# Moving the next graph's node matrix behind conv 1's node product in a two-layer graph network kernel

## The chip, the core and the metric

The kernel runs on one core of one Trainium2 chip. The time is the device time of one execution in microseconds (us). The matrix engine is TensorE (PE, with PEld for its weight loads); the others are VectorE (DVE), ScalarE (ACT), GpSimd (POOL) and the queue of SyncE (SP), which issues the transfers (DMA).

## What is computed

There are 128 graphs. Each has 128 nodes with 512 features (`x`, float32) and a 128x128 adjacency matrix `adj`. Layer 0 is a pair of hypergraph convolutions with a layer norm between them, layer 1 a mean aggregation; both have a layer norm in front and add their result to `x`. Cut to what matters:

```
h = max(layernorm(x), 0)
H = (adj != 0);  w = first row of adj                 # per graph
Dn = 1 / (H @ w);  Be = 1 / column sums of H          # 0 where the sum is 0
conv(v, W, b) = Dn * (H @ (Be * (H.T @ (v @ W.T)))) + b
y = conv(layernorm(relu(conv(h, W1, b1))) * gamma + beta, W2, b2)     # 512 -> 1024 -> 512
x = x + (y + h)
h = max(layernorm(x), 0)
x = x + relu(concat(h, adj @ h / rowsum(adj)) @ W.T)
```

The kernel forms `S = H Be H.T`, a 128x128 matrix of a graph (the **node matrix**), together with the sums `H @ w` as one more column. Conv 1 first multiplies `S` with the features (the **node product**), and then with the weights.

## The kernel before

All weights stay on chip. A product with weights is made of three products of rounded parts (high, low and a correction, letters `h`, `l`, `d`), so that TensorE's faster float32 form can be used; helper `product` (L521) issues them, each with 512 columns, into two PSUM banks (`...m` and `...d`). A pool of six banks serves these, another of two serves the small products `ps_s` (node matrix) and `pz` (node product).

The work of a graph is cut into some eighty small stages (functions under `@stage`), each called with the graph's number. The order of the calls is written out by hand: `head` for the first graphs, `step(s)` for s from 3 to 124, `tail` for the last. Every engine works off its instructions in the order of the calls; a call that waits holds up what is behind it on the same engine only. In one step several graphs are under way: conv 1 of graph s and the start of s + 1, conv 2 of s - 1 and s - 2, layer 1 of s - 3 and s - 4, and the preparation of s + 2. On TensorE a step is, in this order: node matrix of s + 1, second half of conv 1's weights of s (`rm`, `rd`), conv 2's node product of s - 2 (`ym`, `yd`), layer 1's mean weights (`bm`, `bd`), node product of s + 1 (`pz`), layer 1's self weights (`am`, `ad`), conv 2's weights of s - 1 (`gm`, `gd`), the aggregate (into `am`, `ad`), first half of conv 1's weights of s + 1.

The names that the change touches:

- The node matrix's operands come from a chain of small stages. `load_adjb` fetches the adjacency block by block (four transfers on SP's queue), `incidence` (L386) transposes it (`raw`) and compares it with 0 (`adjt`) on DVE, with the column sums; `incidence_weight`, `incidence_count` and `incidence_inverse` prepare two columns (`cnt`), `incidence_high` splits them into high and low, and two calls of `incidence_scale` scale `adjt` by them into `sb`. `node_matrix` multiplies `adjt` and `sb` (258 columns) and copies the first half of the result to `s` on ACT; `node_sum` adds the second half on DVE; `node_floor`, `node_scale` and `node_up` make the factors `dinv` from the last column.
- `conv1_nodes` (L485) issues four products of 128 columns in plain float32, `x_norm` makes its feature operand `h`; `conv1_high`, `conv1_low` and `conv1_rest` split the result into the three parts `z`.
- Layer 1 transposes its input through memory: `layer1_trip_out` writes `h_scratch`, `layer1_trip_in` reads it back in four transfers as `hb`, `layer1_turn` transposes blocks on DVE (`ht`). Conv 2's input goes the same way (`n_scratch`, `nb`, `nt`), and the mean operator (`an_scratch`, `anb`). `finish` makes the output `o` on DVE, `store` sends it out.
- `fill` puts float32 products of constants in front of the next small product, `w1[..].high/low/rest` and `scale_w2` prepare weights in the head.

In the step of before, the node matrix of s + 1 is called early, with operands that were prepared in the middle and at the end of the step before it.

Of the kernel before, what the change touches and what calls it, by code (L numbers as in the profile page):

```python
# [24 lines left out]
def gnn_kernel(  # L25
# [401 lines left out]
    @stage  # L427
    def node_matrix(g):
        PS[g] = ps = small_bank("ps_s")
        nc.tensor.matmul(ps[:, : 2 * P + 2], HT.pop(g), SB.pop(g)[:, : 2 * P + 2], start=True, stop=True)  # L430
        s = small.tile([P, P + 1], FP, tag="s", name="s", bufs=4)
        copy(s, ps[:, : P + 1], AF.Copy, scale=4096.0 if steady(g) else 1.0)
        S[g] = s

# [49 lines left out]
    @stage  # L484
    def conv1_nodes(g):  # L485
        PZ[g] = z = small_bank("pz")
        for k in range(KD):
            nc.tensor.matmul(z[:, k * P : (k + 1) * P], H0[g][:, k * P : (k + 1) * P], S[g],  # L488
                             start=True, stop=True)

# [365 lines left out]
    def step(s):  # L856
        node_high(s - 2)
        conv2_bias(s - 2)
        conv2_high(s - 2)
        layer1_self_main(s - 4)  # L860
        layer1_high(s - 3)
        inner_out(s - 1)
        conv2_low(s - 2, nc.vector)
        x_norm(s + 1)
        node_rest(s - 2)
        conv1_main(s, 0)
        layer1_self_out(s - 4)
        conv2_rest(s - 2)
        node_matrix(s + 1)
        conv1_weights(s, 1)  # L870
        conv1_out(s, 0)
        mean_out(s - 3)
        layer1_low(s - 3)
        layer1_rest(s - 3)
        inner_in(s - 1)
        conv2_nodes(s - 2)
        node_sum(s + 1)
        node_floor(s + 1, nc.gpsimd)
        conv2_out(s - 2)
        conv1_main(s, 1)  # L880
        conv1_out(s, 1)
        inner_turn(s - 1)
        layer1_sums(s - 2)
        mean_in(s - 3)
        layer1_spread(s - 2)
        conv1_bias(s, 0)
        load_adj(s - 2)
        incidence(s + 2)
        layer1_mean(s - 3)
        incidence_weight(s + 2, nc.vector)  # L890
        scales(s - 2, 3)
        layer1_mean_main(s - 3)
        finish(s - 4)
        conv1_bias(s, 1)
        shifts(s - 2, 3, nc.vector)
        conv1_nodes(s + 1)
        store(s - 4)
        load_x(s + 2)
        inner_high(s - 1)
        conv1_high(s + 1)  # L900
        mean_transpose(s - 3)
        layer1_mean_out(s - 3)
        layer1_self(s - 3)
        mean_operator(s - 2)
        inner_low(s - 1, nc.vector)
        inner_rest(s - 1)
        layer1_norm(s - 2)
        inner_sums(s)
        layer1_mean_high(s - 3)
        inner_spread(s)  # L910
        conv2_weights(s - 1)
        layer1_mean_low(s - 3, nc.vector)
        node_scale(s + 1)
        mean_rest(s - 3)
        layer1_trip_out(s - 2)
        x_sums(s + 2)
        incidence_count(s + 2, nc.vector)
        mean_degree(s - 2, nc.vector)
        conv2_main(s - 1)
        scales(s, 2)  # L920
        layer1_mean_rest(s - 3)
        layer1_trip_in(s - 2)
        conv1_low(s + 1)
        incidence_inverse(s + 2)
        residual(s + 1)
        mean_inverse(s - 2)
        conv2_weights_out(s - 1)
        conv1_rest(s + 1)
        shifts(s, 2, nc.gpsimd)
        load_adjb(s + 3)  # L930
        inner_norm(s)
        incidence_high(s + 2)
        layer1_turn(s - 2)
        x_spread(s + 2)
        aggregate(s - 3)
        mean_scale(s - 2, nc.vector)
        incidence_scale(s + 2, 0, nc.vector)
        scales(s + 2, 1)
        conv1_weights(s + 1, 0)
        incidence_scale(s + 2, 1, nc.vector)  # L940
        shifts(s + 2, 1, nc.vector)
        residual_bias(s + 1)
        node_up(s + 1, nc.vector)

    def head():
        load_w1(0, 0)
        load_adjb(0, nc.scalar)
        load_x(1)
        incidence(0)
        copy(eps_root, eps, AF.Sqrt)  # L950
        load_affine()
        load_x(0)
        incidence_weight(0, nc.gpsimd)
        incidence_count(0, nc.vector)
        load_w1(0, 1)
        incidence_inverse(0)
        x_sums(1, "A")
        x_sums(0)
        w1[0].high(0)
        w1[0].high(1)  # L960
        load_x(2)
        load_w1(1, 0)
        w1[0].low(0)
        incidence_high(0)
        x_spread(0)
        scales(0, 1)
        incidence_scale(0, 0, nc.gpsimd)
        incidence_scale(0, 1, nc.scalar)
        load_w1(1, 1)
        w1[0].low(1)  # L970
        w1[0].rest(1, nc.vector)
        load_adjb(1)
        shifts(0, 1, nc.gpsimd)
        x_norm(0)
        node_matrix(0)
        fill(768)
        w1[1].high(1)
        load_w2(0)
        node_sum(0)
        incidence(1)  # L980
        conv1_nodes(0)
        w1[1].high(0)
        residual(0)
        node_floor(0, nc.vector)
        incidence_count(1, nc.vector)
        load_adjb(2)
        w1[0].rest(0, nc.vector)
        x_spread(1)
        load_bias(b2_bc, b2)
        load_bias(b1_bc, b1)  # L990
        w1[1].low(1)
        incidence_inverse(1)
        conv1_high(0)
        conv1_low(0)
        conv1_rest(0)
        node_scale(0)
        incidence_weight(1, nc.gpsimd)
        conv1_weights(0, 0)
        incidence_high(1)
        w1[1].low(0)  # L1000
        incidence_scale(1, 0, nc.scalar)
        w1[1].rest(0, nc.vector)
        incidence_scale(1, 1, nc.scalar)
        load_adj(0)
        node_up(0, nc.scalar)
        conv1_main(0, 0)
        scales(1, 1)
        load_w2(1)
        node_matrix(1)
        shifts(1, 1, nc.gpsimd)  # L1010
        incidence(2)
        node_sum(1)
        incidence_count(2, nc.gpsimd)
        beta_row(0)
        conv1_out(0, 0)
        w1[1].rest(1, nc.vector)
        x_sums(2)
        beta_row(1)
        conv1_weights(0, 1)
        incidence_weight(2, nc.vector)  # L1020
        node_floor(1, nc.gpsimd)
        x_spread(2)
        scale_w2(0, nc.vector)
        scales(2, 1)
        x_norm(1)
        beta_row(2)
        load_x(3)
        shifts(2, 1, nc.gpsimd)
        incidence_inverse(2)
        conv1_bias(0, 0, nc.vector)  # L1030
        scale_w2(1, nc.scalar)
        w2[0].high(0)
        beta_row(3)
        incidence_high(2)
        conv1_nodes(1)
        load_adjb(3)
        scale_w2(2, nc.vector)
        conv1_main(0, 1)
        load_w3(1)
        mean_operator(0)  # L1040
        node_scale(1)
        scale_w2(3, nc.scalar)
        incidence_scale(2, 0, nc.vector)
        incidence_scale(2, 1, nc.scalar)
        w2[0].high(1)
        conv1_out(0, 1)
        residual_bias(0)
        conv1_high(1, True)
        node_matrix(2)
        conv1_bias(0, 1, nc.vector)  # L1050
        beta_row(4)
        beta_row(5)
        x_norm(2)
        node_sum(2)
        conv1_nodes(2)
        mean_degree(0, nc.vector)
        node_up(1, nc.gpsimd)
        node_floor(2, nc.vector)
        inner_sums(0)
        inner_spread(0)  # L1060
        residual(1)
        node_scale(2)
        residual(2)
        load_adjb(4)
        conv1_low(1)
        scale_w2(5, nc.vector)
# [3 lines left out]
        incidence_weight(3, nc.gpsimd)  # L1070
        conv1_rest(1)
        incidence_count(3, nc.gpsimd)
        scales(0, 2)
        incidence_inverse(3)
        conv1_low(2)
        beta_row(6)
        shifts(0, 2, nc.vector)
        beta_row(7)
        w2[1].high(0)
        conv1_rest(2)  # L1080
        incidence_high(3)
        w2[0].low(1)
        unit()
        scale_w2(6, nc.vector)
        inner_norm(0)
        x_sums(3)
        scale_w2(7, nc.scalar)
        w2[0].low(0)
        mean_inverse(0)
        w2[1].low(0)  # L1090
        node_up(2, nc.scalar)
        incidence_scale(3, 0, nc.vector)
        w2[1].high(1)
        conv1_weights(1, 0)
        conv1_weights(1, 1)
        incidence_scale(3, 1, nc.scalar)
        conv1_main(1, 0)
        conv1_main(1, 1)
        inner_out(0)
        w2[0].rest(0)  # L1100
        inner_in(0)
        conv1_out(1, 0)
        x_spread(3)
        w2[0].rest(1)
        conv1_out(1, 1)
        conv1_bias(1, 0, nc.vector)
        conv1_bias(1, 1, nc.vector)
        inner_sums(1)
        node_matrix(3)
        conv1_weights(2, 0)  # L1110
        scales(3, 1)
        incidence(4)
        w2[1].low(1)
        inner_spread(1)
        w2[1].rest(1, nc.gpsimd)
        incidence_weight(4, nc.vector)
        load_x(5)
        inner_turn(0)
        beta_out()
        scales(1, 2)  # L1120
        conv1_weights(2, 1)
        incidence_count(4, nc.gpsimd)
        inner_high(0)
        shifts(1, 2, nc.scalar)
        node_sum(3)
        inner_norm(1)
        w3[1].high(1)
        w3[1].high(0)
# [432 lines left out]
```

## Time and profile before

| what | value |
| --- | --- |
| median of 3 runs (lowest to highest) | 2449.39 us (2448.46 to 2452.33) |
| the profiled execution | 2447.67 us |
| its span, from first to last instruction | 2445.9 us |
| granted TensorE clock | 1.0 |
| node matrix `ps_s`, TensorE | 128 products of 258 columns |
| node product `pz`, TensorE | 1024 records of 128 columns |
| HBM traffic over the span | 126 GB/s |

A profile is one execution. Its page gives the busy time of each engine, the span in 40 slices, the chain of waits that ended last, and groups of equal instructions. The time line gives instructions in order of their start, equal ones merged (x4 is four of them), with the start in us from the span's start. Records of a matrix product overlap, since products are pipelined, so what one costs is read from its start to the start of the next. The windows view gives the busy time of all engines in a stretch.

### The profile page before, as it was taken

To read this page: it belongs to the slowest core of one execution; us is meant where nothing else is said; L and a number is where in the kernel's file an instruction comes from. 1 tells how busy PE (TensorE), PEld (TensorE's weight loads), DVE (VectorE), ACT (ScalarE), POOL (GpSimd) and SP (SyncE) were. 2 spreads that over 40 slices of the span, in tenths; PEclk is the share of its full clock that TensorE was granted. 3 is DMA by queue.
4 is the path that set the end of the run, shared out by engine and by line. 5 is a ranking of instruction groups with operands and counts; after the bars stand their busy time and mean duration, and the time that the engine had idled before them with its cause. 6 is when DMAs were issued, how large, how long until landed. Compare 5 with 4: busy or idle time off the path is not lost.

```text
span 2445.9 us, 41647 instructions
## 1 busy us (share of the span) xinstructions
PE 2422.7 (99%) x11170; PEld 2009.6 (82%) x11170; DVE 2298.1 (94%) x5843; ACT 2009.9 (82%) x4512; POOL 1324.8 (54%) x1808
## 2 busy tenths in 40 slices
PE   7999999999999999999999999999999999999998
PEld 5788888888888888888888888888888888888886
DVE  8899999999999999999999999999999999999987
ACT  8888888888888888888888888888888888888785
POOL 5555555555555555555555555555555555555552
PEclk9999999999999999999999999999999999999999
DMA  6344433344434443444344443434343444344432
GB/s 186 114 129 125 130 124 129 124 130 128 129 119 130 132 126 123 129 129 127 124 128 128 126 129 123 132 123 130 122 133 121 130 127 131 119 131 131 127 124 92
DMA packets 408956, 311.39 MB, mean 127 GB/s; under 512 B 176656, under 2 KB 339984, under 8 KB 408720
## 3 DMA queue, kind: packets, MB, share of 16 engines
q1 hardware_dynamic: 407888, 308.66, 40.1%
q8 instruction: 88, 1.44, 0.2%
q14 instruction: 148, 1.21, 0.2%
q10 hardware_dynamic: 576, 0.07, 0.0%
q0 software_dynamic: 256, 0.01, 0.0%
HBM read 166.21 MB, written 142.34 MB: 126 GB/s over the span
## 4 chain that ended last, share of the span: by engine, by line
PE 95%; ACT 2%; DVE 1%; DMA 1%; issue 1%; SPq 0%; POOL 0%; POOLq 0%; DVEq 0%; ACTq 0%
PE gm L530 19%; PE rm L530 18%; PE am L530 9%; PE bm L530 9%; PE gd L535 9%; PE rd L535 9%; PE bd L535 5%; PE ad L535 5%; PE pz L488 4%; PE am L832 2%; PE ad L832 1%; PE ym L743 1%; PE yd L744 1%; PE ym L742 1%; PE ps_s L430 1%
## 5 line engine op out<-in xcount | busy, mean ns | idle before, releaser
L306 ACT ACTIVATE h<-x_t 128x512 f32<-128x512 f32 x255 | 159.1, 624 | 291.8 <-DVE x_t L754 283.8
L81 POOL TENSOR_TENSOR r<-r,b_bc 128x256 f32<-128x256 f32 x500 | 358.7, 739 | 70.1 <-DVE r L555 54.4
L300 POOL TENSOR_SCALAR st<-st 128x1 f32<-128x1 f32 x130 | 82.3, 633 | 569.9 <-DVE st L317 563.2
L81 POOL TENSOR_TENSOR hl<-ht,hh 128x256 fp32r<-128x256 f32 x250 | 235.4, 963 | 216.5 <-ACT hh L612 216.5
L81 POOL TENSOR_TENSOR x_t<-x_t,h 128x256 f32<-128x256 f32 x256 | 239.8, 959 | 1.3 <-ACT h L326 1.1
L81 POOL TENSOR_TENSOR g<-g,c 128x256 f32<-128x256 f32 x246 | 177.6, 743 | 72.4 <-DVE g L694 72.4
L326 ACT ACTIVATE h<-x_t,st 128x512 f32<-128x512 f32 x255 | 206.1, 808 | 2.0 <-POOL st L300 1.2
L555 DVE SCALAR_TENSOR_TENSOR r<-rd,dinv,r 128x512 f32<-128x512 f32 x256 | 190.8, 746 | 7.7 <-ACT r L550 6.3
L81 POOL TENSOR_TENSOR x_t<-x_t,b_bc 128x256 f32<-128x256 f32 x256 | 187.2, 752 | 0.0
L311 ACT ACTIVATE h<-x_t,st 128x512 f32<-128x512 f32 x255 | 182.9, 717 | 4.1
L550 ACT ACTIVATE r<-rm,dinv 128x512 f32<-128x512 f32 x256 | 174.7, 684 | 7.7 <-PE rm L530 4.4
L694 DVE SCALAR_TENSOR_TENSOR g<-gd,g 128x512 f32<-128x512 f32 x127 | 87.8, 691 | 79.5 <-issue 70.4
L621 DVE SCALAR_TENSOR_TENSOR nd<-nh,nl 128x1024 fp32r<-128x1024 f32 x127 | 155.5, 1225 | 4.2
L326 ACT ACTIVATE r<-r,st 128x1024 f32<-128x1024 f32 x128 | 157.8, 1233 | 0.1
L591 DVE STREAM_TRANSPOSE nt<-nb 128x1024 f32<-128x1024 f32 x127 | 156.9, 1235 | 0.4 <-DMA nb<-n_scratch 0.3
L81 DVE TENSOR_TENSOR nl<-nt,nh 128x1024 fp32r<-128x1024 f32 x127 | 153.5, 1208 | 1.9 <-ACT nh L612 1.7
L530 PE MATMUL am<-w31h,hh 128*128 128x512 f32 x504 | 146.8, 413 | 0.0
L311 ACT ACTIVATE junk<-r,st 128x1024 bf16<-128x1024 f32 x128 | 145.2, 1134 | 0.1
L488 PEld LDWEIGHTS pz<-s,h 128*128 128x128 f32 x1024 | 134.5, 192 | 11.1 <-ACT h L326 0.7
L530 PE MATMUL rm<-w11h,z 128*128 128x512 f32 x512 | 140.3, 396 | 0.0
L530 PE MATMUL rm<-w11l,z 128*128 128x512 f32 x512 | 139.3, 393 | 0.0
L530 PE MATMUL rm<-w10h,z 128*128 128x512 f32 x512 | 138.2, 392 | 0.9 <-ACT z L501 0.9
(244 smaller groups left out, 7594.1 us busy)
## 6 DMA issues: line engine op xcount, KB each, us to landing
n_scratch<-r SPq DMA_DIRECT2D x128, 512.0 KB, 2.6
nb<-n_scratch SPq DMA_DIRECT2D x508, 128.0 KB, 2.8
x_t<-in_x_dram SPq DMA_DIRECT2D x128, 256.0 KB, 2.7
h_scratch<-h SPq DMA_DIRECT2D x127, 256.0 KB, 2.3
hb<-h_scratch SPq DMA_DIRECT2D x508, 64.0 KB, 1.9
out_dram<-o SPq DMA_DIRECT2D x127, 256.0 KB, 2.0
adj_t<-in_adj_dram SPq DMA_DIRECT2D x128, 64.0 KB, 1.9
an_scratch<-adj_t SPq DMA_DIRECT2D x128, 64.0 KB, 1.6
```

The costliest lines, as they stand in the source:

```text
L81: eng.tensor_tensor(dst[:, s], a[:, s], b[:, s], op)
L306: copy(junk, src, func, accum_out=t[:, 0:1])
L311: copy(junk, src, AF.Square, bias=t[:, 1:2], accum_out=t[:, 2:3])
L326: copy(dst, src, func, bias=t[:, 5:6], scale=t[:, 4:5])
L488: nc.tensor.matmul(z[:, k * P : (k + 1) * P], H0[g][:, k * P : (k + 1) * P], S[g], start=True, stop=True)
L530: nc.tensor.matmul(pm, left[i](k), right(i, k), start=(i == 0 and k == 0), stop=(i == 1 and k == kk - 1))
L535: nc.tensor.matmul(pd, left[2](k), right(2, k), start=(k == 0), stop=(k == kk - 1), skip_group_check=True)
L550: copy(R[g][:, HALVES[half]], PY.pop((g, half)), AF.Copy, scale=DN[g][:, 1:2])
L555: nc.vector.scalar_tensor_tensor(r, PR.pop((g, half)), dn[:, 0:1], r, MUL, ADD)
L591: nc.vector.transpose(nt.rearrange("p k (i b) -> p k i b", b=B), t.rearrange("p i k a -> p k i a"))
L621: nc.vector.scalar_tensor_tensor(t, h, 2.0**-12, low, MUL, SUB)
L694: nc.vector.scalar_tensor_tensor(G[g], PG.pop(g), 4096.0, G[g], MUL, ADD)
```

## The change

`node_matrix` becomes a wrapper of a plain function `matrix`, and `conv1_nodes` calls it for the next graph directly behind its own four products, for graphs 4 to 125 (N is 128):

```diff
-    @stage
-    def node_matrix(g):
+    def matrix(g):
         PS[g] = ps = small_bank("ps_s")
         nc.tensor.matmul(ps[:, : 2 * P + 2], HT.pop(g), SB.pop(g)[:, : 2 * P + 2], start=True, stop=True)
...
+    @stage
+    def node_matrix(g):
+        matrix(g)
...
             nc.tensor.matmul(z[:, k * P : (k + 1) * P], H0[g][:, k * P : (k + 1) * P], S[g],
                              start=True, stop=True)
+        if 4 <= g <= N - 3:
+            done.add((node_matrix.f, g + 1))
+            matrix(g + 1)
```

So in step s the node matrix of graph s + 2 is formed behind the node product of s + 1. The list of calls in `step` is a new one. The chain from `incidence` to `incidence_scale` of graph s + 2 moves to its front half, `node_sum(s + 2)` to its end, and the other calls are rearranged as well. On TensorE a step is now: second half of conv 1's weights of s, conv 2's node product, layer 1's mean weights, layer 1's self weights, node product of s + 1, node matrix of s + 2, conv 2's weights, the aggregate, first half of conv 1's weights of s + 1. The new list:

```
        node_high(s - 2)
        conv1_weights(s, 1)
        inner_out(s - 1)
        conv2_bias(s - 2)
        conv2_high(s - 2)
        layer1_self_main(s - 4)
        node_rest(s - 2)
        conv2_low(s - 2, nc.vector)
        layer1_high(s - 3)
        conv2_rest(s - 2)
        conv2_nodes(s - 2)
        layer1_self_out(s - 4)
        conv1_main(s, 0)
        x_norm(s + 1)
        conv1_out(s, 0)
        layer1_low(s - 3)
        incidence(s + 2)
        inner_in(s - 1)
        conv1_main(s, 1)
        layer1_rest(s - 3)
        conv2_out(s - 2)
        node_floor(s + 1, nc.gpsimd)
        mean_out(s - 3)
        layer1_mean(s - 3)
        conv1_out(s, 1)
        incidence_count(s + 2, nc.gpsimd)
        layer1_mean_main(s - 3)
        layer1_self(s - 3)
        incidence_weight(s + 2, nc.gpsimd)
        load_adj(s - 2)
        incidence_inverse(s + 2)
        layer1_sums(s - 2)
        inner_turn(s - 1)
        conv1_bias(s, 0)
        incidence_high(s + 2)
        mean_in(s - 3)
        finish(s - 4)
        layer1_spread(s - 2)
        scales(s - 2, 3)
        conv1_bias(s, 1)
        store(s - 4)
        incidence_scale(s + 2, 1, nc.scalar)
        mean_operator(s - 2)
        residual(s + 1)
        shifts(s - 2, 3, nc.vector)
        incidence_scale(s + 2, 0, nc.vector)
        inner_high(s - 1)
        layer1_norm(s - 2)
        inner_sums(s)
        load_adjb(s + 3)
        layer1_mean_out(s - 3)
        inner_low(s - 1, nc.vector)
        layer1_mean_high(s - 3)
        mean_transpose(s - 3)
        mean_degree(s - 2, nc.vector)
        node_scale(s + 1)
        inner_rest(s - 1)
        load_x(s + 2)
        inner_spread(s)
        layer1_mean_low(s - 3, nc.vector)
        mean_rest(s - 3)
        mean_inverse(s - 2)
        layer1_trip_out(s - 2)
        conv1_nodes(s + 1)
        scales(s, 2)
        shifts(s, 2, nc.gpsimd)
        layer1_trip_in(s - 2)
        conv1_high(s + 1)
        conv2_weights(s - 1)
        conv2_main(s - 1)
        inner_norm(s)
        mean_scale(s - 2, nc.vector)
        layer1_mean_rest(s - 3)
        residual_bias(s + 1)
        node_up(s + 1, nc.vector)
        conv1_low(s + 1)
        conv2_weights_out(s - 1)
        x_sums(s + 2)
        x_spread(s + 2)
        conv1_rest(s + 1)
        aggregate(s - 3)
        node_sum(s + 2)
        layer1_turn(s - 2)
        scales(s + 2, 1)
        shifts(s + 2, 1, nc.vector)
        conv1_weights(s + 1, 0)
```

Three small operations of the chain change their engine in a step: count and weight go from DVE to POOL, one of the two scales from DVE to ACT. `head` and `tail` are rearranged too. Of the head's beginning, what differs most:

```diff
     def head():
+        load_adjb(0, nc.scalar)
+        load_x(0)
         load_w1(0, 0)
-        load_adjb(0, nc.scalar)
+        w1[0].high(0)
         load_x(1)
         incidence(0)
+        load_w1(0, 1)
         copy(eps_root, eps, AF.Sqrt)
         load_affine()
...
-        fill(768)
+        fill(1152)
...
+        fill(256)
```

Both `head` and `tail` issue the same weight products as before; the order of some of them changes, and so does the engine of some small operations. ACT loads one more table in the head.

## The prediction

> **What bounds the kernel now.** I read the page first: busy times, then the chain that ended last.
>
> ```profile
> PE 2422.7 (99%) x11170; PEld 2009.6 (82%) x11170; DVE 2298.1 (94%) x5843; ACT 2009.9 (82%) x4512; POOL 1324.8 (54%) x1808
> ...
> PE 95%; ACT 2%; DVE 1%; DMA 1%; issue 1%; SPq 0%; POOL 0%; POOLq 0%; DVEq 0%; ACTq 0%
> ```
>
> TensorE is busy in 99% of the span and makes 95% of the chain. A busy share is an average, so I asked for windows: the head, one step in the middle, the end of the tail (columns: stretch, its length, then the busy time of PE, PEld, DVE, ACT and POOL, granted clock, DMA share, GB/s).
>
> ```profile
> 16.88:105.25 88.37, 85.82 (x369) 65.70 (x370) 79.19 (x177) 79.55 (x173) 44.35 (x65) 1.00 0.50 141
> ...
> 2409.70:2445.90 36.20, 28.25 (x115) 20.24 (x113) 25.21 (x47) 15.28 (x32) 3.75 (x6) 1.00 0.24 77
> 1209.41:1228.15 18.74, 18.74 (x88) 15.65 (x87) 17.90 (x47) 15.50 (x36) 10.33 (x14) 1.00 0.40 128
> ```
>
> A step of 18.74 us has 18.74 us of PE: no hole at all. VectorE is next with 17.90, so it has 0.84 us to spare. Only the head (with the 16.88 us before its first weight product) and the tail have PE holes. So the middle gets faster only where PE's own sum gets smaller, and slower only where something comes later than its cover. Now PE's order in that step (start, length, line, tiles, count):
>
> ```profile
> 1212.13 0.28 PE L430 MATMUL ps_s<-sb,adjt 128*128 128x258 f32 x1
> 1212.25 1.09 PE L530 MATMUL rm<-w11h,z 128*128 128x512 f32 x4
> ...
> 1215.02 0.39 PE L742 MATMUL ym<-gp,sp 128*128 128x512 f32 x1
> ...
> 1218.42 1.05 PE L488 MATMUL pz<-s,h 128*128 128x128 f32 x8
> 1219.22 1.17 PE L530 MATMUL am<-w31h,hh 128*128 128x512 f32 x4
> 1220.23 1.07 PE L530 MATMUL am<-w31l,hl 128*128 128x512 f32 x4
> ```
>
> Lengths overlap; I count from start to start. Four products of 512 columns take 0.907 (0.227 each). From `ps_s` to `ym` are 2.89 us, twelve such products are 2.72: the node matrix costs 0.17, though 258 columns at that rate are 0.114. The node product `pz` takes 0.80 to the next start, and the group behind it 1.01 instead of 0.907: 0.90 in all.
>
> **PE's order.** Each step keeps its 78 products of 512 columns, its `pz` and its `ps_s`. `ps_s` leaves its place between two weight products of conv 1 and comes behind `pz`, for 122 graphs (5 to 126). Is it cheaper there? The trace has no `pz` followed by `ps_s` without a wait. The nearest rows:
>
> ```profile
> 40.26 0.28 PE L430 MATMUL ps_s<-sb,adjt 128*128 128x258 f32 x1
> 40.38 1.08 PE L530 MATMUL rm<-w10h,z 128*128 128x512 f32 x4
> ...
> 43.11 0.39 PE L530 MATMUL rm<-w11h,z 128*128 128x512 f32 x1
> ```
>
> ```profile
> 2356.87 0.28 PE L430 MATMUL ps_s<-sb,adjt 128*128 128x258 f32 x1
> 2356.99 1.02 PE L738 MATMUL py<-g,s 128*128 128x512 f32 x2
> ...
> 2360.61 0.39 PE L530 MATMUL bm<-w30h,hh 128*128 128x512 f32 x1
> ```
>
> In the head it costs 2.85 - 2.72 = 0.13. In the tail it stands beside a plain fp32 product: 3.74 - 2.72 = 1.02 for both, and a lone `py` at 2394.74 costs 0.90, which leaves 0.12. The Trainium skill ("TensorE: Matmul & The Clock Gate", Back-to-back issue gap) speaks against the change: an isolated gap is the columns over 2.4 GHz plus 2.5 ns, 110 ns for 258 columns (an estimate from the page) wherever it stands, so a move is worth 0. The rows show 0.17, 0.13 and 0.12 by place, and 227 ns where the page's form gives 216, so I go by the rows. Ends: 0 (the excess goes along to the next weight product), and 0.05 x 122 = 6 us. A loss by an exposed weight load (188 ns against passes 0.11 apart in `pz`) would be 0.08 x 122 = 10 us, but `am` behind `pz` stands in the same place and shows no such gap. I take 0.03, the head's row, since it too is followed by a product of the same kind: **-3.7 us**.
>
> **The waits of `ps_s`.** It now needs its operand in its own step, and behind it on PE stand conv 2's weights, the aggregate and conv 1's first half: all of PE. With 0 at the start of conv 1's first product (1209.41), PE reaches: second half 2.72, `ym` 5.4, `bm` 6.1, `am` 8.8, `pz` 11.6, `ps_s` 12.4, `gm` 12.6. On VectorE I laid the new order out with the old start-to-start times: the low part of conv 2's operand waits for ScalarE as now (2.49), its rest 3.1, `o` 3.8, `r` 4.4, the adjacency's transpose 5.1 and comparison 5.4, `hd` 5.6, the two `x_t` 6.2 and 7.1, `r` 7.7, inverse 8.4, `nt` 8.5, `sb`'s low 9.6, `finish` 9.9, three small ones, `sb`'s scale 11.3, done 11.5. ScalarE's half of `sb` is done near 10.3. So 0.9 us to spare: cost 0. The same list has `nl` done at 13.2 (needed 14.4), `nd` 15.0 (16.2), `hd` 6.2 (7.9); `z`'s rest again directly behind `g<-gd`, 0.9 before its product, as now.
>
> **Work that changes engine.** Per step VectorE loses the weight (0.06 from start to start), the count (0.06) and one 128x128 scale (0.18), 0.30 in all: idle time, worth 0 now. GpSimd gets two of 0.21 (it idles 8 us a step), ScalarE one of about 0.28 (15.5 of 18.74 busy): cost 0.
>
> **SP's queue.** Now the row of this step is:
>
> ```profile
> 1220.75 0.36 SPq L853 DMA_DIRECT2D out_dram<-o  x1
> 1221.15 0.43 SPq L282 DMA_DIRECT2D x_t<-in_x_dram  x1
> 1222.37 0.32 SPq L576 DMA_DIRECT2D h_scratch<-h  x1
> 1224.90 1.92 SPq L584 DMA_DIRECT2D hb<-h_scratch  x4
> 1226.87 1.37 SPq L274 DMA_DIRECT2D adjb<-in_adj_dram  x3
> ```
>
> The four `adjb` issues (0.46 each) move ahead of `x_t` and of layer 1's trip. The trip's write can then not go out before 13.6 (now 13.0): store at 11.0, then 0.4 + 1.8 + 0.4. It lands about 2.3 later, the four reads go out by 18.0, and the last lands near 0.8 of the next step, where VectorE wants it at 1.0: 0.2 left, and 0.25 more because the low part behind it waits for ScalarE anyway. `n_scratch` now goes ahead of `an_scratch`, which delays nobody. Cost 0, with the thinnest cover of all.
>
> **Head and tail.** The head is written anew. ScalarE begins with half of a weight's high part, which waits for its 512 KB (5.2 us from issue), and a second table load (1.28) is needed after it. 6.0 + 1.0 (high) + 1.3 + 0.2 + 1.0 (sums) + 1.2 (spread) + 1.0 (next sums) + 0.2 + 1.0 (second high) + 0.4 (scale) puts the first `ps_s` at 13.3 instead of 11.4. The longer filler (1152 columns instead of 768) lies under the wait for `h`; the new one of 256 under a wait of 0.5 that is there now. ScalarE is busy 79.55 of the next 88.37 us, so much of the 1.9 stays; against it, the 2.55 us of PE holes there may close. Ends -1 and +3; I take **+1.5**. The tail has the same products, and its waits of 0.98 and 1.67 us before `py` are chains of latency that keep their stages: 0, ends -1.5 and +1.5.
>
> **Sum.** -3.7 + 1.5 + 0 = -2.2 us. The profiled execution took 2447.67 (span 2445.9 and 1.8 around it): 2445.5. The median of the runs shown is 1.7 above it, so **2447.2 us**.
>
> **Rivals.**
> - Full saving: all of 0.05 per step and a head that closes its holes: -6 - 1 = -7 us, 2442. For it: the `py` row. Against it: what follows `ps_s` stays a weight product. Chance 0.22.
> - Slower: SP's loop. `finish` to store to `adjb`, `x_t`, trip, `ht`, and down VectorE's list to the next `finish` is a circle: 8.5 us from the end of `finish` to the landing, 9.7 from `ht` to the next `finish`'s end, 18.1 in all. It decides from the point where it exceeds the PE step of 18.7, that is, when something in it grows by 0.6. If the reads land after 2.7 us, as `nb`'s do, instead of 1.9, it stands at 18.9: 0.2 x 122 = 24 us, 2473. For it: four issues were put in the circle. Against it: it needs all of the growth at once in every step. Chance 0.22.
> - A late node chain or a worse head: `sb` later by over 0.9, or the head's 3 and the tail's 1.5 with no saving at `ps_s`: +5 to +8, near 2456. Chance 0.11.
> - The forecast: 0.45, with its own range from 2442 to 2454.
>
> Runs of this kernel tell 0.2% (4.9 us) from no change. Faster takes the first rival and a little of the forecast, 0.25; slower nearly all of the two after it, 0.32; within 0.2%, 0.43. The range for 8 in 10 reaches down to the full saving and up into the loop's smaller excesses: 2440 to 2466.
>
> **What would show it.** Right: a step of 18.70 to 18.72, no wait of PE in the middle, `ps_s` to `gm` near 0.12 and `gm`'s first group at most 0.03 long, VectorE near 17.6 busy a step, first `ps_s` near 13. Wrong: steps longer than 18.75; VectorE waiting for `hb` in every step (the loop); PE waiting for `sb` (the chain); or a middle that is unchanged with `gm`'s groups long by what `rm`'s are now.

## The result, and the profile after

The changed kernel takes 2562.28 us (median of 5 runs, 2557.07 to 2567.16) against 2449.39 (5 runs, 2448.46 to 2452.33): ratio 1.0461, interval 1.0443 to 1.048. It is 113 us slower. The forecast of 2447.2 and its range up to 2466 missed.

The page of the changed kernel: busy times; the chain that ended last, by engine and by line; one row of the transfers (the last number is the median time from issue to landing).

```profile
PE 2493.7 (97%) x11174; PEld 2005.8 (78%) x11174; DVE 2270.0 (89%) x5488; ACT 2067.7 (81%) x4632; POOL 1446.6 (56%) x2041
...
DVE 36%; PE 22%; DMA 14%; ACT 13%; SPq 8%; issue 7%; DVEq 0%; ACTq 0%; POOL 0%; POOLq 0%
DMA h_scratch<-h 8%; PE gm L536 6%; DVE r L561 5%; DMA hb<-h_scratch 5%; PE rm L536 5%; SPq L274 4%; DVE nt L597 4%; DVE x_t L760 4%; SPq L590 3%; DVE o L844 3%; PE gd L541 3%; DVE hd L627 2%; PE rd L541 2%; DVE o L850 2%; DVE ht L597 2%
...
h_scratch<-h SPq DMA_DIRECT2D x127, 256.0 KB, 3.1
```

TensorE still shows 97%, which read alone would say that little happened. The chain says otherwise: TensorE had 95% of it and now has 22%. What holds the chain is layer 1's trip through memory (`h_scratch`, `hb`), SP's loads (L274 among them) and VectorE's list. A high busy share does not name the bound: nearly the same products (11174 records against 11170) now count 2493.7 us of busy time instead of 2422.7, so part of that 97% is not work.

The windows view of the changed kernel (head, one step from conv 1's first product to the next, tail; columns as before):

```profile
0.00:84.87 84.87, 69.51 (x289) 51.37 (x290) 70.27 (x150) 73.42 (x156) 43.53 (x67) 1.00 0.59 160
1207.37:1227.28 19.91, 19.57 (x89) 15.58 (x87) 17.70 (x44) 15.85 (x37) 11.55 (x17) 1.00 0.40 118
2488.40:2560.50 72.10, 63.84 (x276) 50.24 (x275) 56.02 (x107) 43.07 (x88) 18.91 (x28) 0.99 0.31 99
```

The head is 84.87 us long (before 83.55, to the same product), the tail 72.1 (72.8). The loss is in the steps. From the starts of conv 1's first product I worked out the mean of the 122 steps of each trace: 18.77 us before, 19.70 after. The 122 steps together are 114.0 us longer, the head 1.3 longer and the tail 0.7 shorter: 114.6, by which the spans differ too. The granted clock stays at 0.99 to 1.00.

Inside that step, PE's order around the moved product:

```profile
1219.67 1.05 PE L491 MATMUL pz<-s,h 128*128 128x128 f32 x8
1220.93 0.36 PE L429 MATMUL ps_s<-sb,adjt 128*128 128x258 f32 x1 [0.21 <-ACT nh L618]
1221.13 1.09 PE L536 MATMUL gm<-w20h,nh 128*128 128x512 f32 x4
1222.06 1.07 PE L536 MATMUL gm<-w21h,nh 128*128 128x512 f32 x4
```

From `pz` to `ps_s` are 1.26 us; undisturbed it is 0.81 (shown further down). So `ps_s` does wait. The row puts it down to ScalarE's `nh`, which `ps_s` does not read. In 116 steps of the middle `ps_s` starts 0.145 to 0.147 us after VectorE has written its half of `sb`, every time, while its distance to the end of `nh` varies and is once negative. TensorE waits for VectorE here. Is VectorE's list too long, then, or does it start late? VectorE, same stretch, four of its rows:

```profile
1210.21 0.71 DVE L597 STREAM_TRANSPOSE ht<-hb 128x512 f32<-128x512 f32 x1 [1.77 <-DMA hb<-h_scratch]
...
1219.43 0.68 DVE L850 SCALAR_TENSOR_TENSOR o<-o,x_t 128x512 f32<-128x512 f32 x1
...
1220.41 0.38 DVE L300 TENSOR_SCALAR sb<-adjt,sb 128x128 fp32r<-128x128 f32 x1
...
1229.80 0.71 DVE L597 STREAM_TRANSPOSE ht<-hb 128x512 f32<-128x512 f32 x1 [1.29 <-DMA hb<-h_scratch]
```

It starts late: it stands idle for 1.77 and 1.29 us until layer 1's reads (`hb`) have landed, and everything behind `ht` is late by that. SP's queue between the two `ht` shows why:

```profile
1220.14 0.36 SPq L859 DMA_DIRECT2D out_dram<-o  x1
1220.54 1.88 SPq L274 DMA_DIRECT2D adjb<-in_adj_dram  x4
1222.47 0.43 SPq L282 DMA_DIRECT2D x_t<-in_x_dram  x1
1223.00 0.38 SPq L582 DMA_DIRECT2D h_scratch<-h  x1
1226.37 1.75 SPq L590 DMA_DIRECT2D hb<-h_scratch  x4
```

Read the five rows as one line of dominoes. `finish` ends at 1220.11; the store goes out at once, then without a gap four adjacency loads, `x_t` and the write: 2.89 us. From the write to the first read, which waits for its landing, are 3.37 us. The four reads take 1.75 to issue, and the last lands and lets `ht` go 1.68 later. That is 9.69 from the end of `finish` to `ht`, and from `ht` to the end of the next `finish` 9.90 (1210.21 to 1220.11). One turn is 19.59 us, 0.9 above what TensorE needs. It is a circle, so no engine can work off the excess.

The waits of VectorE and ScalarE say that this is no single case (total, times, longest):

```profile
DVE ht L597 <- DMA hb<-h_scratch: 133.6, 94, 2.9
...
ACT g L696 <- DMA h_scratch<-h: 87.9, 109, 2.9
...
PEld ps_s L429 <- ACT nh L618: 36.1, 106, 1.0
```

Before, VectorE waited for `hb` four times:

```profile
DVE ht L591 <- DMA hb<-h_scratch: 3.1, 4, 1.4
```

### The profile page after: what moved, and what is told of

Its sections match the earlier page's. It is cut to its first block, busy times and chain, and to the rows that moved or that the text cites. A ratio compares the mean times of both kernels' runs of the same rounds, so it can differ in the third digit from the quotient of the medians.

```text
span 2560.5 us, 41656 instructions
## 1 busy us (share of the span) xinstructions
PE 2493.7 (97%) x11174; PEld 2005.8 (78%) x11174; DVE 2270.0 (89%) x5488; ACT 2067.7 (81%) x4632; POOL 1446.6 (56%) x2041
## 4 chain that ended last, share of the span: by engine, by line
DVE 36%; PE 22%; DMA 14%; ACT 13%; SPq 8%; issue 7%; DVEq 0%; ACTq 0%; POOL 0%; POOLq 0%
DMA h_scratch<-h 8%; PE gm L536 6%; DVE r L561 5%; DMA hb<-h_scratch 5%; PE rm L536 5%; SPq L274 4%; DVE nt L597 4%; DVE x_t L760 4%; SPq L590 3%; DVE o L844 3%; PE gd L541 3%; DVE hd L627 2%; PE rd L541 2%; DVE o L850 2%; DVE ht L597 2%
## 5 line engine op out<-in xcount | busy, mean ns | idle before, releaser
L300 POOL TENSOR_SCALAR st<-st 128x1 f32<-128x1 f32 x126 | 101.7, 807 | 506.5 <-DVE st L317 504.4
L807 ACT ACTIVATE gb_t<-bm 128x512 f32<-128x512 f32 x127 | 76.1, 599 | 250.1 <-PE bm L536 249.7
L81 POOL TENSOR_TENSOR x_t<-x_t,h 128x256 f32<-128x256 f32 x256 | 249.5, 994 | 0.3 <-ACT h L326 0.2
L597 DVE STREAM_TRANSPOSE ht<-hb 128x512 f32<-128x512 f32 x127 | 90.4, 711 | 173.9 <-DMA hb<-h_scratch 133.6
L696 ACT ACTIVATE g<-gm 128x512 f32<-128x512 f32 x127 | 76.1, 599 | 103.4 <-DMA h_scratch<-h 87.9
L536 PE MATMUL bm<-w30h,hh 128*128 128x512 f32 x504 | 145.9, 411 | 2.7
L541 PE MATMUL rd<-w10d,z 128*128 128x512 f32 x512 | 140.0, 395 | 5.9 <-DVE z L514 5.5
```

What stands on the lines that cost most here:

```text
L81: eng.tensor_tensor(dst[:, s], a[:, s], b[:, s], op)
L536: nc.tensor.matmul(pm, left[i](k), right(i, k), start=(i == 0 and k == 0), stop=(i == 1 and k == kk - 1))
L541: nc.tensor.matmul(pd, left[2](k), right(2, k), start=(k == 0), stop=(k == kk - 1), skip_group_check=True)
L597: nc.vector.transpose(nt.rearrange("p k (i b) -> p k i b", b=B), t.rearrange("p i k a -> p k i a"))
```

## The experiments

The expectations speak of three theories. **L**: SP's loop, just described, sets the step. **C**: the node chain comes too late for its product behind `pz`, and that is the cause rather than a consequence. **M**: the node matrix is dear behind the node product.

### 1. One line moved: the adjacency loads behind layer 1's trip

```diff
-        load_adjb(s + 3)
         layer1_mean_out(s - 3)
...
         layer1_trip_in(s - 2)
+        load_adjb(s + 3)
```

> The changed kernel with one call moved in the step: the four adjacency loads go behind layer 1's trip (its write and its four reads) on SP's queue, as they stood in the kernel before. Theory L (the loop: finish, store, four adjacency loads, x, trip write, trip reads, ht, VectorE's list, next finish sets the step): the loop loses 1.9 us of issues and some 0.8 us of landing, falls under TensorE's 18.75 us, and the time falls to 2445 to 2475, with VectorE's wait for hb gone. Theory C (the node chain is now too late for its product, TensorE waits for sb): nothing of it is touched, 2535 to 2565. Theory M (the node matrix is dear behind the node product): 2535 to 2565.

2471.67 us, ratio 1.0091 (1.0074 to 1.0108): 91 of the 113 us are gone, with the node matrix still behind the node product. Most steps are 18.71 us, some 19 to 20. What is left is a new wait, made by the new place:

```profile
ACT r L556 <- DMA n_scratch<-r: 56.8, 63, 2.2
```

The loads now stand ahead of conv 2's write `n_scratch`; it goes out near 1.3 us of a step, where the kernel of before had 0.5, and the buffer `r` that it reads comes free late for ScalarE's next cast.

### 2. Then x's load earlier

```diff
         conv1_bias(s, 1)
+        load_x(s + 2)
         store(s - 4)
...
         inner_rest(s - 1)
-        load_x(s + 2)
```

> As the run before, and the load of x moves ahead of the store as well, so that the trip's write stands directly behind the store. Theory L: the loop was under TensorE's step already, so no further gain: within 6 us of the run before. If the loop were still the bound there, a further 0.4 us a step, 50 us. Theories C and M: 2535 to 2565.

2495.5 us in a single run: 24 more than the run before, a clear miss. Two transfer rows of its page hold the hint that was needed:

```profile
h_scratch<-h SPq DMA_DIRECT2D x127, 256.0 KB, 3.0
...
out_dram<-o SPq DMA_DIRECT2D x127, 256.0 KB, 3.2
```

The store of the output lands in 2.0 us in the kernels before and after. Here it is issued 0.4 us behind `x_t` and takes 3.2, and the write to `h_scratch`, 1.1 us behind the store, takes 3.0. A write right behind another 256 KB on SP's queue lands late.

### 3. The loads early, in the kernel of before

```diff
         store(s - 4)
+        load_adjb(s + 3)
         load_x(s + 2)
...
         shifts(s, 2, nc.gpsimd)
-        load_adjb(s + 3)
```

> The kernel before with one call moved: the four adjacency loads stand between the store and the load of x, ahead of layer 1's trip, as in the changed kernel. Theory L: VectorE's list from ht to the end of finish is 10.3 us there and the transfers from there to the landing 9.9 us as in the changed kernel, 20.1 us a step instead of 18.75: near 2600 (2540 to 2630). Theories C and M: the node chain and its place are those of before, 2445 to 2455.

2602.81 us in a single run. The old kernel with its old node matrix gets slower too, and by more, when the loads are put ahead of layer 1's trip. Its write lands in 3.2 us instead of 2.3, and again it goes out 0.5 us behind `x_t`. The joining isn't needed for the loss.

### 4. The joining undone in the kernel of after

```diff
-        if 4 <= g <= N - 3:
-            done.add((node_matrix.f, g + 1))
-            matrix(g + 1)
...
     def step(s):
         node_high(s - 2)
+        node_matrix(s + 1)
         conv1_weights(s, 1)
...
         layer1_self_out(s - 4)
+        node_sum(s + 1)
...
-        node_sum(s + 2)
```

> The changed kernel with the joining undone: the node matrix of graph s + 1 stands again ahead of the second half of conv 1's weights in the next step, its sum behind the self product's output; all else, SP's queue too, as changed. Theory L: the loop is the same, 2545 to 2575. Theory C: TensorE has six us more before it needs sb, so its waits go: 2455 to 2490. Theory M: 2450 to 2480.

2568.32 us in a single run: the loss stays when the joining goes, and so does VectorE's wait for the trip (133.6 us in the changed kernel):

```profile
DVE ht L594 <- DMA hb<-h_scratch: 165.1, 101, 3.1
```

By itself this run does not clear C and M, since the place given to the product here has a price of its own: run 10, with SP's loop out of the way, takes 2518.47 us. What clears them are the runs in which the products stay joined and the loss goes: run 1 for most of it, runs 5, 9 and 12 for all of it.

### 5 to 7. The loads in SP's idle wait, and the order on ScalarE

To run 1's kernel, the loads put where SP waits for `n_scratch` anyway (those of graph s + 2 now, so the head loads one fewer and the tail one more):

```diff
         inner_out(s - 1)
+        load_adjb(s + 2)
...
-        load_adjb(s + 3)
```

> As the first run (adjacency behind layer 1's trip, 2471.7 us), but the four loads, now those of graph s + 2, issue right behind n_scratch's store at about 1.3 us of the step, where SP stands idle for that store's landing until 4.0; nothing of SP's queue then lies ahead of n_scratch or h_scratch but x's load and the output's store. Loop theory (L): what was left over the 18.71 us step in the first run (ACT's r waiting 0.4 us a step for n_scratch's landing) goes or shrinks: 2445 to 2460 us. Rival W: the n_scratch store now shares the DMA engines with the four loads behind it and lands as late as before or later, so that nb and with it the other trip come late: 2470 us or more.

And to run 1's kernel, ScalarE's order of before:

```diff
+        x_norm(s + 1)
         conv1_main(s, 0)
-        x_norm(s + 1)
```

> As the first run (2471.7 us), but ScalarE's x_norm ahead of conv 1's first main cast, as in the kernel before: it fills the time in which that cast waits for the buffer that n_scratch's store reads. L with the leftover in that wait: 2450 to 2464 us. If the leftover lies in VectorE's chain or in layer 1's trip instead: within 5 us of 2471.7.

Both together:

> The fifth and sixth run's edits together. L: the step is TensorE's undisturbed 18.71 us, 0.04 less than before's 18.75, over 122 steps 5 us, the head 1.3 us longer, the tail 0.7 shorter: 2445 us (2442 to 2455). If the idle-wait placement delays n_scratch's landing (W): 2465 us or more.

The first gives 2447.41 us (ratio 0.9988, 0.9981 to 0.9995): L's figure, and under the kernel of before. SP's queue of that kernel:

```profile
1211.96 0.34 SPq L582 DMA_DIRECT2D n_scratch<-r  x1
1212.34 2.18 SPq L274 DMA_DIRECT2D adjb<-in_adj_dram  x4
1214.71 1.73 SPq L590 DMA_DIRECT2D nb<-n_scratch  x4
```

The four loads fill the 2.4 us between the write's issue and the first read that waits for it; the write still lands in time. Nothing else had to move.

The second is a miss: 2483.98 us (ratio 1.013, 1.0117 to 1.0144), 12 above run 1. The wait that it was to cover shrank (56.8 to 21.9 us), but another came:

```profile
DVE r L561 <- ACT r L556: 54.2, 105, 2.2
...
DVE ht L597 <- DMA hb<-h_scratch: 26.9, 37, 1.6
```

VectorE now waits 105 times for conv 1's cast, which stands behind `x_norm` (33 times and 30.8 us in run 1). That it loses there what ScalarE saved is read from the waits, not tested. The third is a miss for the same edit: 2455.5 us (1.0021, 1.0015 to 1.0028), 8 above the kernel without it.

### 8 and 9. The loads on another queue

```diff
-        load_adjb(s + 3)
+        load_adjb(s + 3, nc.gpsimd)
```

> After with the four adjacency loads at their place, but issued by GpSimd's queue: SP's 1.9 us of issue goes, the transfers stay where they are in time and share the engines with x and h_scratch as before. L with the issue time as the price: below 2480 us. L with the landing (contention on the engines) as the price: 2500 to 2555 us. GpSimd has 44% of its time free; if its own issues delay its tiles (cnt, sp), the step is over 19 us by another wait, named by the waits of GpSimd's readers.

> The eighth run's kernel again (after with the four adjacency loads issued by GpSimd's queue, 2447.28 us in one look), timed in rounds: does it lie under before? Step 18.71 in 115 of 117 steps of its trace against 18.75, head 1.3 us longer: L expects 2446 to 2449, ratio to before 0.9985 to 0.9995. If the one look was a lucky one: 2450 to 2460.

2447.28 us in a single run, 2446.37 as the median of 21 (ratio 0.9985, 0.9979 to 0.9992). The transfers are the same, at nearly the same time; only SP no longer issues them, so that `x_t` and the write move apart as well (1.5 us instead of 0.5). GpSimd issues them, in a gap that it had, and a step is whole again. GpSimd's rows (time line) and the step's window in the second of the two:

```profile
1219.20 1.96 POOL L81 TENSOR_TENSOR x_t<-x_t,h 128x256 f32<-128x256 f32 x2
1221.11 2.22 POOL L274 DMA_DIRECT2D adjb<-in_adj_dram  x4
1225.48 0.86 POOL L300 TENSOR_SCALAR st<-st 128x1 f32<-128x1 f32 x1 [2.15 <-DVE st L317]
```

```profile
1209.02:1227.73 18.71, 18.71 (x88) 15.66 (x87) 17.53 (x44) 15.79 (x37) 13.37 (x21) 1.00 0.40 126
```

PE is busy for all of 18.71 us, and here the joined products can be seen undisturbed:

```profile
1220.58 1.05 PE L491 MATMUL pz<-s,h 128*128 128x128 f32 x8
1221.39 0.37 PE L429 MATMUL ps_s<-sb,adjt 128*128 128x258 f32 x1
1221.59 1.09 PE L536 MATMUL gm<-w20h,nh 128*128 128x512 f32 x4
1222.52 1.07 PE L536 MATMUL gm<-w21h,nh 128*128 128x512 f32 x4
```

By the medians of all steps these are 0.808 + 0.203 + 0.927 = 1.938 us. Before, the same three cost 0.808 + 1.004 + 0.160 = 1.972, in two places: 0.034 us a step.

### 10 and 11. What the joining itself is worth

The kernel with the loads on GpSimd's queue, joining undone as in run 4:

> The eighth run's kernel with the joining alone undone (the node matrix back at the front of the next step, node_sum with it), so that the change's own idea is priced with SP's loop out of the way. By the profiles the joined products save 0.04 us a step (18.71 against 18.75): 2450 to 2455 us, 5 above the joined one. Theory C or M in a small form (the product behind the node product costs TensorE time): at or below the joined kernel, 2440 to 2447.

2518.47 us (ratio 1.0281, 1.0266 to 1.0295), a miss by 64 us. Nearly every step is 19.3. ScalarE's rows at the front of a step:

```profile
1209.37 0.28 ACT L431 ACTIVATE s<-ps_s 128x129 f32<-128x129 f32 x1 [0.51 <-PE ps_s L429]
1209.55 0.62 ACT L709 ACTIVATE gp<-g 128x512 fp32r<-128x512 f32 x1
```

The cast of `s` waits 0.51 us for the product, and `gp`, `hh` and all of ScalarE's queue wait behind it; this wait occurs 118 times. So the place was wrong, if that is what costs the time, and the run says nothing of the joining. The next one tests it. On TensorE the product stays where it was, directly ahead of the second half of conv 1's weights; the calls move together, so that the cast of `s` comes between ScalarE's two casts of `r`, as in the kernel of before:

```diff
-        node_matrix(s + 1)
-        conv1_weights(s, 1)
...
-        conv2_nodes(s - 2)
         layer1_self_out(s - 4)
-        node_sum(s + 1)
         conv1_main(s, 0)
+        node_matrix(s + 1)
+        conv1_weights(s, 1)
+        conv2_nodes(s - 2)
+        node_sum(s + 1)
```

> As the tenth run, but the node matrix between the two halves of conv 1's second product, so that ScalarE's cast of s stands between its two main casts, as in the kernel before, and not at the front of its queue, where it held hh and the casts behind it 0.5 to 1.2 us up. If the tenth run's loss was that place: 2449 to 2455 us, and the difference to the joined kernel (2446.4) is the joining's own worth, 0.04 us a step or 5 us in all. If the loss comes with any separate node matrix in this order: above 2480 us.

2454.46 us (1.0019, 1.0011 to 1.0027), as expected: run 10's loss was the place. Its step is 18.75 in nearly all cases, against 18.71 with the products joined; unrounded the medians are 0.034 apart. The spans differ by 7.7 us (2451.7 to 2444.0), of which 0.034 x 122 = 4.1 are the joining; most of the rest is eight steps of over 19 us in this kernel, against one, and why they are long stays open.

### 12. Which part of the circle grew

By now the landing of the write followed the gap between `x_t`'s issue and the write's (medians of each trace, adjacency loads on SP's queue):

| kernel | from `x_t`'s issue to the write's | write lands after |
| --- | --- | --- |
| after | 0.5 us | 3.1 us |
| run 1 | 1.1 | 2.4 |
| before | 1.2 | 2.3 |
| run 5 | 1.5 | 2.2 |

Runs 3 and 4 (0.5 us, 3.2) and runs 6 and 7 (1.1, 2.4) fit as well. Run 2 does not by this gap alone: there the late store stands between `x_t` and the write.

The page's row of before:

```profile
h_scratch<-h SPq DMA_DIRECT2D x127, 256.0 KB, 2.3
```

By these numbers it is `x_t`, and not the four loads, that the write waits behind. The last run tells the two apart: the loads stay ahead of the write, and only `x_t` goes behind it.

```diff
         inner_rest(s - 1)
-        load_x(s + 2)
...
         layer1_trip_out(s - 2)
+        load_x(s + 2)
```

> After, with only x's load moved: it stands right behind layer 1's write to h_scratch and no longer right ahead of it; the four adjacency loads stay ahead of the write. In the runs so far the write's landing follows the gap from x's issue to the write's: 0.5 us gives 3.1, 1.05 gives 2.4, 1.24 gives 2.3, 1.49 gives 2.2. If x's 256 KB are what the write waits behind: it lands 2.2 to 2.6 after its issue, the circle is under 18.7 us, and the time is 2446 to 2465 us. If the four small loads are what it waits behind: it still lands near 3.1, the write only goes out 0.5 us sooner, the circle is 19.1 and the time 2480 to 2500 us.

2446.74 us (ratio 0.999, 0.9983 to 0.9997). One line moved takes the whole loss away. SP's queue, and the transfer row of its page:

```profile
1219.24 0.36 SPq L859 DMA_DIRECT2D out_dram<-o  x1
1219.64 1.88 SPq L274 DMA_DIRECT2D adjb<-in_adj_dram  x4
1221.62 0.37 SPq L582 DMA_DIRECT2D h_scratch<-h  x1
1222.33 0.35 SPq L282 DMA_DIRECT2D x_t<-in_x_dram  x1
1224.01 1.75 SPq L590 DMA_DIRECT2D hb<-h_scratch  x4
```

```profile
h_scratch<-h SPq DMA_DIRECT2D x127, 256.0 KB, 2.0
```

The write goes out 2.40 us after `finish` (1219.22) with all four loads ahead of it, and the first read follows 2.39 later instead of 3.37. Two terms of the circle lose 0.49 and 0.98; 19.59 - 1.47 = 18.12 us, under TensorE's 18.71, and the circle no longer decides. `x_t` is issued in the time in which SP waits for the landing anyway. Whether `x_t` would hold the write up as much from another queue, by use of the same DMA engines and not by its place, no run here tells.

Three kernels thus lie under both: 2446.37 (loads on GpSimd's queue), 2446.74 (`x_t` behind the write) and 2447.41 (loads in the idle wait). Their intervals overlap; which is best is not settled.

## Why the prediction was wrong

**The step that failed** is "SP's queue", which ends "Cost 0, with the thinnest cover of all"; the real cost was all of the loss. The mechanism had been written down as the rival "Slower: SP's loop", with its point of decision: the circle stood at 18.1 us and "decides from the point where it exceeds the PE step of 18.7, that is, when something in it grows by 0.6". It grew by 1.5. Term by term, in the stretch shown:

| term of the circle | predicted | measured |
| --- | --- | --- |
| end of `finish` to the write's issue | 2.6 us | 2.89 |
| write's issue to the first read | 2.3 | 3.37 |
| issue of the four reads | 2.1 | 1.75 |
| to `ht` | 1.5 | 1.68 |
| `ht` to the end of the next `finish` | 9.7 | 9.90 |
| sum | 18.1-18.2 | 19.59 |

The term that carries it is the second. "It lands about 2.3 later" was a figure of before, taken where SP had 1.22 us between `x_t`'s issue and the write's. The same text moved the four loads ahead of `x_t`, so that store, loads, `x_t` and write go out back to back, and then kept the old landing: 2.3 us where 3.37 were measured. The last run shows it: the same loads ahead, `x_t` out of the way, and the write lands in 2.0. The Trainium skill says what was overlooked ("DMA: Bandwidth & Descriptors", Queues, rings and completion order): on each DMA engine the descriptors of one queue are consumed in order. The table above agrees, with 3.1 us behind `x_t` by 0.5 and 2.2 by 1.5.

**The rival had the right circle, too much room and the wrong transfer.** Its last term, 9.7, does not agree with the same text's time line, where `ht` starts at 1.0 and the store goes out at 11.0: 10.0 us, so the circle stood at 18.5 and the room was the 0.2 that "SP's queue" names, not 0.6. It let the reads land after 2.7 us instead of 1.9 and came to 2473. The reads take 2.0. What grew was the write, and the queue ahead of it was only 0.3 of the growth. The objection "it needs all of the growth at once in every step" was no objection: an order written out by hand is the same in every step.

**PE's order** was right in its sum, by luck. -0.03 a step was forecast, and -0.034 came out in the kernels where nothing else disturbs it. But the parts differ from the text. It expected a cheaper `ps_s`, 0.13; it is dearer, 0.20. The saving comes from the 0.10 that a weight group paid directly behind `pz`: the group that now follows `ps_s` takes only 0.02 more than its 0.907. The sum left this term out, and does not agree with the text's own signs: `ps_s` at 0.12 and that group at most 0.03 long would be a saving of 0.1. Row and rule gave -3.7 and 0 us; the two kernels of the same order with and without the joining, -4.1 by their usual steps.

**The waits of `ps_s`** were right in the undisturbed kernels: no wait, `sb` done 0.85 us ahead of the product (0.9 forecast). In the changed kernel they appear, as a consequence of the late `ht`. A reader who stops at TensorE's own waits would blame the joining.

**Work that changes engine** at nothing: right. VectorE is busy 17.53 us of a step (17.6 forecast), and GpSimd even had room for the four issues.

**Head and tail.** +1.5 forecast, +1.3 measured; 0 forecast, -0.7 measured. The head's number is in part luck: the first `ps_s` comes at 12.11 us, not at the 13.3 of the text (11.40 before). More is lost behind it: ScalarE puts both pieces of the next weight's high part ahead of `h`, and the first real `pz` starts at 16.28 instead of 14.31. The tail's -0.7 belongs to the changed kernel with its late trip. In the last run, with the loss gone, the trace has +1.9 in the head, -4.5 in the 122 steps and +0.9 in the tail, -1.7 in all, each part inside its forecast ends. The forecast without the loop was -2.2, and the times of that run differ by as much (2446.74 against 2448.99, timed side by side).

## What to carry to other kernels

A trip through memory that ends where it began is a circle, and its length is compared with the step as one sum: when an edit puts anything into it, add up all of it again with the new neighbours, not with the old durations. A transfer's time from issue to landing belongs to what stands ahead of it on its queue, so take it from a row with the same gap, and put loads that nobody waits for into the queue's own wait, behind the write and ahead of the reads. Undo the disputed edit at a place where its side effects are known: runs 4 and 10 measured the place (ScalarE's queue) instead of the edit.

## What the runs showed of the hardware

- A 256 KB write issued 0.5 us behind a 256 KB load on the same queue landed in 3.1 us, 1.5 us behind it in 2.2, with the load behind it in 2.0, although four 16 KB loads stood directly ahead of it. An output store 0.4 us behind the same load took 3.2 instead of 2.0.
- The same four loads on GpSimd's queue cost it 0.56 us of issue each (0.47 on SP's), and the write that ran beside them landed in 2.5 us (run 9) where it took 2.2 without (run 5), in both 1.5 us behind `x_t`.
- The node matrix (258 columns, operands in the faster float32 form, as the row of `sb` shows) costs 0.16 us between two weight products, and between `pz` and a weight product 0.20 and 0.02 more in the group behind it. The whole is still 0.034 cheaper, because a weight group directly behind the plain float32 `pz` took 1.004 us instead of 0.907.
